# Graph attention on one core: the softmax denominators leave PSUM through ScalarE, and two VectorE steps change places

## The chip, the core and the metric

The kernel runs on one NeuronCore of a Trainium2 chip. A core has five engines that run side by side, each through its own instructions in order: TensorE (PE in the profile; matrix products, whose results go to PSUM), VectorE (DVE), ScalarE (ACT), GpSimd (POOL) and SyncE (SP, which here issues transfers). [...] The metric is the device time of one launch in microseconds (us), lower is better; before the change it is 3842.06 us, the median of three runs from 3838.66 to 3844.71.

## The reference

Two layers on 32 graphs of 512 nodes with 512 features. All graphs share one adjacency matrix `adj` (512 x 512, about 3% ones). Each layer adds something to its input and normalises the rows.

```python
# layer 0: message passing
deg = adj.sum(axis=1)
out = deg[None, :, None] * (x @ Wi.T + b) + einsum('ij,bjo->bio', adj, x @ Wj.T)
x = layernorm(x + out)

# layer 1: attention with 8 heads of 64, masked by adj
q, k, v = split_heads(h @ Wq.T + bq), split_heads(h @ Wk.T + bk), split_heads(h @ Wv.T + bv)
scores = where(adj == 0, -inf, einsum('bhqd,bhkd->bhqk', q, k) / 8)
out = einsum('bhqk,bhkd->bhqd', softmax(scores), v)       # heads merged again
x = layernorm(x + out @ Wo.T + bo)
```

The layer bias of layer 0 enters as `deg * b`, one row times one column.

## The kernel before

One program handles the graphs one after the other, with three of them in work at once: while the scores of graph `b` are computed, the attention output of `b-1` is projected, and layer 0 and the projections q, k, v of `b+1` are made. A period, one graph's worth of this, has eight score steps (two head groups of four key blocks). At each step TensorE computes the scores of two head pairs, the product with the values for the step before, and then a share of the projections, which come as "pieces" (L427) of sums and differences of quarters of the matrices.

**The softmax.** Scores are made with keys on the partitions, so the mask is a multiplication after the exponential, and the denominators are sums over partitions, done by TensorE with a matrix of ones:

```python
    def scores(b, hp, kc):
        ps = sc_tile()                                    # [128, 2, 512] in PSUM, bufs=2
        for s in range(2):
            r = slice(s * HD, (s + 1) * HD)
            nc.tensor.matmul(ps[:, s, :], KT[...][r, ...], QT[...][r, ...], start=True, stop=True)   # L481
        e = E[hp % 2, kc] = work([P, 2, N], "e", 4)
        nc.scalar.activation(ps, ps, AF.Exp, scale=QSCALE)                                           # L485
        nc.vector.tensor_tensor(e, ps, edge[...], op=OP.mult)                                        # L486

    def values(b, g, kc):                                 # L503: e times v, into PV[g], two banks "ov"
        ...
    def sums(g, kcs=(1,), last=1):
        if g not in RL:
            RL[g] = (sc_tile()[:, 0, :], work([P, N], "rl", 1))   # takes one of the two score tiles
        ...                                                       # L513: ones times es, into RL[g][0]

    def invert(g, part):
        pl, rl = RL[g]
        c = slice(part * P, (part + 1) * P)
        nc.vector.reciprocal(rl[:, c], pl[:, c])                                                     # L518

    def tell(b, g):
        pl, rl = RL.pop(g)
        j = b * 2 + g
        nc.vector.tensor_tensor_reduce(pl, pl, rl, 1.0, 0.0, OP.add, OP.add, told[:, j:j + 1])       # L523

    def scale(b, g, r, c=slice(0, N)):
        ...
        nc.vector.tensor_mul(OT[b, g][:, r, c], PV[g][r][:, c], RL[g][1][:, c])                      # L528

    def rest(b, g):
        return [(invert, g, c) for c in range(4)] + [(scale, b, g, 0), (scale, b, g, 1), (tell, b, g)]
```

`tell` adds up denominators and reciprocals, so that at the end the kernel can see whether a number ran out of range; a slower general path then takes over. The masked exponentials of the key blocks are added up ahead (`presum`: L492 on GpSimd, L494 on VectorE, tile `es`), so that the sums need one pass.

**Layer 0.** x arrives twice: in rows (`XT`) and in blocks that VectorE's transpose turns into columns (`XA`, turned into `XD`). The product with `adj` uses a split of x into two parts, made from `XT`:

```python
    def split(b, dc):
        xs = XT[b][:, :, dc * P:(dc + 1) * P]
        nc.scalar.copy(hi, xs)                                                                       # L203
        nc.gpsimd.tensor_sub(lo, xs, hi.bitcast(FT))                                                 # L204, tile xlo

    def l0_gather(b, dc, bank, adjT=None):                # L325: products, L331: copy out, then split(b, dc + 2)
        ...
    def l0_turn(b, dc):
        nc.vector.transpose(XD[b][:, dc, :], XA[b][:, dc, :])                                        # L339
        nc.gpsimd.tensor_tensor(XD[b][:, dc, :], XD[b][:, dc, :], deg_r, op=OP.mult)                 # L340

    def base(b, half):                                    # the layer bias, two blocks of rows
        for ic in range(2 * half, 2 * half + 2):
            y = XT[b][:, ic, :]
            nc.vector.scalar_tensor_tensor(y, b0_r, deg_c[:, ic:ic + 1], y, op0=OP.mult, op1=OP.add) # L345
```

**h.** The output of layer 0 goes to memory and comes back in blocks, to be turned in two halves; GpSimd forms differences of its quarters for the pieces:

```python
    def h_turn(b, half):
        nc.vector.transpose(HT[b][:, :, Q * half:Q * half + Q], HA[b][:, half])                      # L373, reads tile xa
    def combos(T, b, quarters, which, part=None):         # L396: GpSimd, tile big
        ...
```

**The order.** Lists of small functions lay down the order of a period; `g` are the gathers, `k` pieces of the k projection:

```python
    def phase_a(n):
        ...
        for i in range(DC):
            res += g[i:i + 1] + k[i:i + 1] + [z(l0_turn, n, i)]
            ...
        return res + [z(combos, TX, n, xq, (2,)), z(combos, TA, n, aq, (2,)), z(base, n, 0),
                      z(combos, TX, n, xq, (3, 4)), z(combos, TA, n, aq, (3, 4)), z(base, n, 1),
                      pc("l0", n, 1, A), k[4]]

    def phase_c(n):
        ...
            res = [z(apply, n, 1), z(h_store, n, 1), v[1], *project(m, 3), z(h_load, n, 1), z(stats, m, 0), v[2], z(stats, m, 1),
                   q[1], k[1], z(apply, m, 0), q[2], z(apply, m, 1), z(store, m), z(h_turn, n, 1),
                   z(combos, TH, n, h, (1, 2)), z(combos, TH, n, h, (3, 4)), k[2]]
```

The main loop puts them between the steps:

```python
        for step in range(STEPS):
            scores(b, 2 * g, kc)
            scores(b, 2 * g + 1, kc)
            ...
                values(pb, pg, pk)
                if pk == NC - 1:                          # the group's last key block
                    sums(pg)
                    extra = rest(pb, pg)
            ...                                           # then the pieces of this step, with `extra` between them
```

Of the kernel before, what the change touches and what calls it, by code (L numbers as in the profile page):

```python
# [9 lines left out]
FT = mybir.dt.float32  # L10
# [3 lines left out]
AF = mybir.ActivationFunctionType  # L14
OP = mybir.AluOpType
AX = mybir.AxisListType

P = 128
# [3 lines left out]
SAFE = 1e18  # L22
# [3 lines left out]
def gnn_attention_kernel(  # L26
# [36 lines left out]
    nc = tc.nc  # L63
    B, N, D = x.shape
# [8 lines left out]
    const = ctx.enter_context(tc.tile_pool(name="const", bufs=1))  # L73
# [6 lines left out]
    def work(shape, name, bufs, dtype=FT):  # L80
        return pools.work.tile(shape, dtype, name=name, bufs=bufs)

    def big():
        return work([P, 4, N], "big", 6)
# [7 lines left out]
    def sc_tile():  # L92
        return psum.tile([P, 2, N], FT, name="sc", bufs=2)
# [9 lines left out]
    TX, TA, TH, TO = {}, {}, {}, {}  # L103
# [68 lines left out]
    adj_f = big()  # L172
# [11 lines left out]
        return t  # L184


    told = const.tile([P, B * 2 + 1], FT, name="told")
    adjR = const.tile([P, NC, N], FR, name="adjR")
    adjT = turned(adj_f, big(), adjR)
    deg_r = const.tile([P, N], FT, name="deg_r")  # L190
# [35 lines left out]
    def graph_forms(part):  # L226
        if part == 3:
            nc.vector.reduce_sum(deg_c, adj_f, axis=AX.X)
        elif part == 0:
            nc.vector.tensor_tensor(adj_f, adjT, adjR.bitcast(FT), op=OP.not_equal)  # L230
        elif part == 1:
            nc.vector.reduce_sum(told[:, B * 2:], adj_f.rearrange("p c i -> p (c i)"), axis=AX.X)
            nc.vector.tensor_scalar(told[:, B * 2:], told[:, B * 2:], 2.0 * SAFE, None, op0=OP.mult)
        else:
            nc.vector.tensor_scalar(edge, adjT, 0.0, None, op0=OP.not_equal)

# [144 lines left out]
    def quarter(src, j, n):  # L381
        return src[:, 2 * j:2 * j + 2, Q * n:Q * n + Q]
# [92 lines left out]
    E, ES, PV, RL = {}, {}, {}, {}  # L475
# [30 lines left out]
    def sums(g, kcs=(1,), last=1):  # L506

        if g not in RL:
            RL[g] = (sc_tile()[:, 0, :], work([P, N], "rl", 1))
        for kc in kcs:  # L510
            for h in range(4):
                src = ES[h // 2] if kc == 1 else E[h // 2, kc]
                nc.tensor.matmul(RL[g][0][32 * h:32 * h + 32, :], ones[:, :32], src[:, h % 2, :], start=(kc == 1), stop=(kc == last))  # L513

    def invert(g, part):
        pl, rl = RL[g]
        c = slice(part * P, (part + 1) * P)
        nc.vector.reciprocal(rl[:, c], pl[:, c])  # L518

    def tell(b, g):  # L520
        pl, rl = RL.pop(g)
        j = b * 2 + g
        nc.vector.tensor_tensor_reduce(pl, pl, rl, 1.0, 0.0, OP.add, OP.add, told[:, j:j + 1])  # L523

    def scale(b, g, r, c=slice(0, N)):
# [4 lines left out]
    def rest(b, g):  # L530
        return [(invert, g, c) for c in range(4)] + [(scale, b, g, 0), (scale, b, g, 1), (tell, b, g)]
# [9 lines left out]
    def z(f, *a):  # L541
        return (0.0, f, *a)

    def pc(kind, b, i, bank):
        return (2 * PC if kind == "l0" else PC, piece, kind, b, i, bank)
# [6 lines left out]
    def banks(n):  # L552

        return ("a", "b") if n % 2 == 0 else ("b", "a")

    def phase_a(n):

        A, K = banks(n)
        if n == B:
            return [pc("k", n - 1, i, bank) for i, bank in ((6, K), (5, A), (7, K), (3, A), (4, K))]  # L560
        xq, aq = lambda j, m: quarter(XD[n], j, m), lambda j, m: quarter(AX_T[n], j, m)
        g = [(GA, l0_gather, n, dc, A) for dc in range(DC)]
        k = [pc("k", n - 1, i, K) for i in LATE]
        res = []
        for i in range(DC):
            res += g[i:i + 1] + k[i:i + 1] + [z(l0_turn, n, i)]
            if n == 1 and i in (1, 3):
                res += [z(combine, "wo", nc.vector, i // 2)]
            if i == 1:
                res += [z(combos, TX, n, xq, (1,)), z(combos, TA, n, aq, (1,))]  # L570
        return res + [z(combos, TX, n, xq, (2,)), z(combos, TA, n, aq, (2,)), z(base, n, 0),
                      z(combos, TX, n, xq, (3, 4)), z(combos, TA, n, aq, (3, 4)), z(base, n, 1),
                      pc("l0", n, 1, A), k[4]]

    def first():
# [25 lines left out]
    def project(m, i):  # L601

        res = [pc("pj", m, i, banks(m)[1])]
        if i == 1:
            res = [z(combos, TO, m, ot_quarter(m), (1,))] + res
        if i == 2:
            res = [FLUSH] + res + [z(combos, TO, m, ot_quarter(m), (2, 3, 4))]
        return res
# [21 lines left out]
    def phase_c(n):  # L630

        m = n - 2
        norm = [(TR, l0_norm, n, ic) for ic in range(NC)]
        h = lambda j, i: quarter(HT[n], j, i)
        A, K = banks(n)
        v, q, k = [{i: pc(kind, n, i, bank) for i in ORDER} for kind, bank in (("v", A), ("q", K), ("k", A))]
        if m < 0:
            res = [v[1]] + ([z(apply, n, 1)] if n else []) + [q[1], v[2], norm[2], norm[3], z(combos, TH, n, h, (1, 2)), k[1],
                                                             z(combos, TH, n, h, (3, 4)), q[2], k[2]]
        else:  # L640
            res = [z(apply, n, 1), z(h_store, n, 1), v[1], *project(m, 3), z(h_load, n, 1), z(stats, m, 0), v[2], z(stats, m, 1),
                   q[1], k[1], z(apply, m, 0), q[2], z(apply, m, 1), z(store, m), z(h_turn, n, 1),
                   z(combos, TH, n, h, (1, 2)), z(combos, TH, n, h, (3, 4)), k[2]]
        side = []
        if n == 0:

            side = [z(graph_forms, 2), None, z(graph_forms, 0), None, z(graph_forms, 1)]
        for i in LATE:
            for f in q[i], v[i]:
                res += [f] + [g for g in side[:1] if g]  # L650
                side = side[1:]
                if i in (6, 7) and 0 < n < B - 1:
                    res += [z(load_xa, n + 1, 2 * (i == 7) + (f is v[i]))]
            if i == 3 and 0 < n < B - 1:
                res += [z(load_x, n + 1)]
            if i == 7 and n + 1 < B:
                res += [z(ahead, n + 1)]
        return res
# [32 lines left out]
    def run(f):  # L691
        f[1](*f[2:])
# [49 lines left out]
    for n in range(1, B + 1):  # L742
        b = n - 1
        extra = []
        for step in range(STEPS):
            g, kc = divmod(step, NC)
            scores(b, 2 * g, kc)
            scores(b, 2 * g + 1, kc)
            pb, pg, pk = (b, *divmod(step - 1, NC)) if step > 0 else (b - 1, 1, NC - 1)
            if pb >= 0:  # L750
                values(pb, pg, pk)
                if pk == NC - 1:
                    sums(pg)
                    extra = rest(pb, pg)
            late = [(presum, i, kc) for i in range(2) if kc > 0]
            if b == B - 1 and kc == 3:
                late = [late[0], late[1] + (nc.gpsimd,)]
            if b == B - 1 and g == 1 and kc > 1:

                late = []  # L760
            for f in PERIODS[n][step]:
                if f is FLUSH:
                    some = len(extra)
                else:
                    run(f)

                    some = 0 if f[0] == 0.0 else len(extra) if step == 0 else max(1, round(f[0] / PC))
                if some:
                    for g in late[:1] + extra[:some]:
                        g[0](*g[1:])  # L770
                    late, extra = late[1:], extra[some:]
            for g in late + extra:
                g[0](*g[1:])
            extra = []
# [4 lines left out]
        last_part(c, 1)  # L779
    for ic in range(NC):  # L780
        c = slice(ic * P, (ic + 1) * P)
        invert(1, ic)
        scale(B - 1, 1, 0, c)
        scale(B - 1, 1, 1, c)
        last_part(2, ic=ic)
        last_part(3, ic=ic)
        if ic > 0:
            last_rows(ic - 1)
    tell(B - 1, 1)
    last_rows(NC - 1)  # L790
    flags()
    fast.close()
    flag = nc.values_load(again[0:1, 0:1], min_val=0, max_val=1)
    with tc.If(flag > 0), tc.tile_pool(name="general", bufs=1) as pools.work:
# [4 lines left out]
        adj_f = big()  # L799
# [21 lines left out]
        with tc.For_i(0, B, 1) as b:  # L821
            g = "general"
# [6 lines left out]
            for ic in range(NC):  # L829
                c = slice(ic * P, (ic + 1) * P)  # L830
# [10 lines left out]
            for ic in range(NC):  # L841
                c = slice(ic * P, (ic + 1) * P)
                nc.vector.tensor_copy(V[g][:, ic, :], product([(HT[g][:, dc, c], wv[:, dc, :]) for dc in range(DC)]))
            for hp in range(HP):
                c = slice(hp * P, (hp + 1) * P)
# [5 lines left out]
                for qb in range(NC):  # L851
# [7 lines left out]
                    for s in range(2):  # L859
# [3 lines left out]
                                            op0=OP.mult, op1=OP.add)  # L863
                    for s in range(2):
                        nc.scalar.activation(pr[:, s, :], pr[:, s, :], AF.Exp, bias=sm[:, 2 + s:3 + s], scale=1.0,
                                             accum_out=sm[:, 4 + s:5 + s])
# [14 lines left out]
            for ic in range(NC):  # L881
                c = slice(ic * P, (ic + 1) * P)
# [45 lines left out]
```

## Time and profile before

| | |
|---|---|
| time, median of three | 3842.06 us |
| span of the profiled execution | 3839.1 us |
| TensorE busy | 3695.2 us, 96% |
| VectorE busy | 2395.5 us, 62% |
| GpSimd busy | 1986.7 us, 52% |
| ScalarE busy | 992.5 us, 26% |
| mean granted clock of TensorE | 0.995 |

In the profile a line such as `PE sc L481 <- DVE told L523: 57.1, 32, 4.4` says: TensorE stood idle ahead of the products of line 481 that write tile `sc`, until VectorE's instruction of line 523 that writes `told` was done; 57.1 us in all, 32 times, at most 4.4 us. In a timeline the columns are start, length, engine, line, operation, output and inputs, shape and number; what stands in brackets is the idle time of the engine before it and who ended it. In a chain, which is followed back from the last instruction, they are start, length and work. `mma` and `mmb` are the two PSUM banks of the pieces, `ring` the tiles through which their weights come.

### The profile page before, as it was taken

Reading aid. Unit: us, or ns where it says so; the run is one execution under the profiler, and the core shown is the slowest. Engines: PE = TensorE matmul, PEld = TensorE weight load, DVE = VectorE, ACT = ScalarE, POOL = GpSimd, SP = SyncE. Lnnn points to the kernel's source line nnn. Section 1 sums busy time; section 2 is a strip of 40 time slices with the busy share of each in tenths; the row PEclk is TensorE's granted clock in tenths of the full one; section 3 lists DMA queues with packets and bytes.
Section 4 is the critical chain, followed back from the end, with each engine's and each line's share of the span. In section 5 each row is a group of like instructions: output and inputs, shape, how many; then the busy total and the mean of one; then the engine's idle time right before and its main releaser. Section 6 shows DMA issues by size and latency. Waiting matters only on the chain.

```text
span 3839.1 us, 49650 instructions
## 1 busy us (share of the span) xinstructions
PE 3695.2 (96%) x18458; PEld 2505.9 (65%) x18458; DVE 2395.5 (62%) x3202; ACT 992.5 (26%) x1356; POOL 1986.7 (52%) x1985
## 2 busy tenths in 40 slices
PE   8999999999999999999999999999999999999997
PEld 5666666666666666666666666666666666666663
DVE  4566666666666666666666666666666666666666
ACT  2222222222222222222222222222222222222222
POOL 3555545555445555455554555644555545555443
PEclk9999999999999999999999999999999999999999
DMA  7444555444554545554445544455544455444541
GB/s 246 133 114 129 138 151 154 129 129 132 140 157 139 132 125 143 147 155 129 127 131 149 151 135 128 131 143 154 144 126 130 139 150 154 128 126 133 145 131 46
DMA packets 797174, 530.03 MB, mean 138 GB/s; under 512 B 530432, under 2 KB 611840, under 8 KB 796928
## 3 DMA queue, kind: packets, MB, share of 16 engines
q1 hardware_dynamic: 780384, 494.78, 47.7%
q10 hardware_dynamic: 16320, 31.46, 2.2%
q8 instruction: 151, 2.47, 0.3%
q14 instruction: 95, 0.78, 0.1%
q0 software_dynamic: 224, 0.53, 0.0%
HBM read 453.25 MB, written 73.40 MB: 137 GB/s over the span
## 4 chain that ended last, share of the span: by engine, by line
PE 81%; DVE 15%; POOL 1%; SPq 1%; issue 1%; ACT 1%; DMA 0%; DVEq 0%; POOLq 0%; ACTq 0%
PE mma L427 27%; PE mmb L427 27%; PE sc L481 10%; PE ov L503 10%; DVE xh L345 4%; PE mmb L325 3%; PE mma L325 3%; DVE e L486 3%; DVE oT L528 1%; PE sc L513 1%; POOL big L396 1%; DVE es L494 1%; DVE big L373 1%; DVE rl L518 1%; ACT sc L485 1%
## 5 line engine op out<-in xcount | busy, mean ns | idle before, releaser
L485 ACT ACTIVATE sc<-sc 128x1024 f32<-128x1024 f32 x512 | 495.7, 1006 | 1703.1 <-PE sc L481 1697.4
L486 DVE TENSOR_TENSOR e<-sc,edge 128x1024 f32<-128x1024 f32 x512 | 604.9, 1217 | 341.1 <-ACT sc L485 315.6
L427 PE MATMUL mmb<-ring,big 128*128 128x256 f32 x3144 | 733.1, 382 | 3.1 <-issue 3.1
L427 PE MATMUL mma<-ring,big 128*128 128x256 f32 x3112 | 727.4, 382 | 4.2 <-ACT p L434 3.0
L427 PEld LDWEIGHTS mmb<-ring,big 128*128 128x128 f32 x3144 | 593.1, 190 | 133.8 <-issue 29.4
L427 PEld LDWEIGHTS mma<-ring,big 128*128 128x128 f32 x3112 | 587.4, 190 | 137.0 <-DVE e L486 26.8
L396 POOL TENSOR_TENSOR big<-big 128x512 f32<-128x512 f32 x376 | 508.1, 1378 | 163.7 <-DVE big L373 144.7
L481 PE MATMUL sc<-q,k 64*128 64x512 f32 x2048 | 521.0, 621 | 57.2 <-DVE told L523 57.1
L503 PE MATMUL ov<-e,v 128*32 128x512 f32 x4096 | 498.5, 605 | 0.0
L427 PE MATMUL mma<-big,ring 128*128 128x256 f32 x1808 | 431.8, 382 | 8.7 <-POOL big L396 8.0
L427 PE MATMUL mmb<-big,ring 128*128 128x256 f32 x1776 | 424.2, 382 | 8.5 <-POOL big L396 8.5
L492 POOL TENSOR_TENSOR es<-e 128x1024 f32<-128x1024 f32 x128 | 302.0, 2360 | 243.8 <-DVE e L486 240.7
L291 POOL TENSOR_SCALAR mv<-mv 128x1 f32<-128x1 f32 x256 | 51.0, 199 | 692.7 <-DVE mv L290 680.2
L427 PEld LDWEIGHTS mma<-big,ring 128*128 128x128 f32 x1808 | 339.2, 190 | 87.3 <-issue 13.8
L427 PEld LDWEIGHTS mmb<-big,ring 128*128 128x128 f32 x1776 | 333.2, 190 | 86.0 <-POOL big L396 14.5
L204 POOL TENSOR_TENSOR xlo<-xh,xhi 128x512 fp32r<-128x512 f32 x128 | 163.8, 1291 | 392.8 <-ACT xhi L203 392.8
L481 PEld LDWEIGHTS sc<-q,k 64*128 64x128 f32 x2048 | 174.6, 186 | 274.9 <-issue 270.3
L503 PEld LDWEIGHTS ov<-e,v 128*32 128x32 f32 x4096 | 107.8, 110 | 354.0 <-issue 354.0
L340 POOL TENSOR_TENSOR big<-big,deg_r 128x512 f32<-128x512 f32 x124 | 197.8, 1595 | 247.0 <-DVE big L339 247.0
L494 DVE TENSOR_TENSOR es<-es,e 128x1024 f32<-128x1024 f32 x251 | 306.8, 1223 | 0.0
L445 DVE TENSOR_TENSOR xh<-xh,mma 128x512 f32<-128x512 f32 x186 | 126.9, 682 | 272.4 <-PE mma L427 272.4
L445 DVE TENSOR_TENSOR xh<-xh,mmb 128x512 f32<-128x512 f32 x186 | 126.8, 682 | 257.9 <-PE mmb L427 257.7
(142 smaller groups left out, 3614.4 us busy)
## 6 DMA issues: line engine op xcount, KB each, us to landing
ring<-wo SPq DMA_DIRECT2D x217, 256.0 KB, 2.8
ring<-wq SPq DMA_DIRECT2D x160, 256.0 KB, 3.1
ring<-wv SPq DMA_DIRECT2D x160, 256.0 KB, 2.7
ring<-wk SPq DMA_DIRECT2D x160, 256.0 KB, 3.1
ring<-wi SPq DMA_DIRECT2D x155, 256.0 KB, 2.7
ring<-wj SPq DMA_DIRECT2D x155, 256.0 KB, 2.6
xh<-in_x_dram SPq DMA_DIRECT2D x32, 1024.0 KB, 5.3
xa<-in_x_dram SPq DMA_DIRECT2D x124, 256.0 KB, 4.0
```

Of the source, the lines that this page charges most:

```text
L204: nc.gpsimd.tensor_sub(lo, xs, hi.bitcast(FT))
L325: nc.tensor.matmul(pm, parts[w][:, jc, :], adjR[:, jc, :], start=(w == 0 and jc == 0), stop=(w == 1 and jc == NC - 1))
L340: nc.gpsimd.tensor_tensor(XD[b][:, dc, :], XD[b][:, dc, :], deg_r, op=OP.mult)
L396: nc.gpsimd.tensor_tensor(dst, p, q, op=OP.subtract)
L427: nc.tensor.matmul(pm[:, c * Q:(c + 1) * Q], lhs, rhs, start=first, stop=(kc == 1 and n == len(terms) - 1), skip_group_check=True)
L445: nc.vector.tensor_tensor(d, d, pm, op=OP.add)
L481: nc.tensor.matmul(ps[:, s, :], KT[b, hp // 2][r, hp % 2, kc * P:(kc + 1) * P], QT[b, hp // 2][r, hp % 2, :], start=True, stop=True)
L485: nc.scalar.activation(ps, ps, AF.Exp, scale=QSCALE)
L486: nc.vector.tensor_tensor(e, ps, edge[:, kc:kc + 1, :].to_broadcast([P, 2, N]), op=OP.mult)
L492: nc.gpsimd.tensor_add(ES[i], E[i, 0], E[i, 1])
L494: (eng or nc.vector).tensor_add(ES[i], ES[i], E[i, kc])
L503: nc.tensor.matmul(PV[g][r][32 * h:32 * h + 32, :], V[b][:, kc, c0:c0 + 32], E[h // 2, kc][:, h % 2, :], start=(kc == 0), stop=(kc == NC - 1))
```

## The change

Three things are moved, none of the mathematics.

1. The denominators are copied from PSUM to the tile `rl` by ScalarE as soon as TensorE has summed them (`drain`), with their sum as a by-product. The reciprocals are then taken in place in `rl`, and `tell` sums the reciprocals alone. The PSUM tile can go back to the scores after the copy. The last group of the last graph, where nothing follows, keeps the old way (`invert(..., 0)`, `tell_all`). `told` has two columns for each group now.
2. `base` stands after the transposes of chunks 1 and 2 of x, not after all four and GpSimd's differences.
3. `h_turn` of the second half stands ahead of a piece of q, which puts it in VectorE's order ahead of the masks of that step instead of behind them.

```diff
-    told = const.tile([P, B * 2 + 1], FT, name="told")
+    told = const.tile([P, B * 4 + 1], FT, name="told")
...
-    def invert(g, part):
-        pl, rl = RL[g]
+    def drain(b, g):
+
+        j = 2 * (b * 2 + g)
+        nc.scalar.activation(RL[g][1], RL[g][0], AF.Identity, accum_out=told[:, j:j + 1])
+
+    def invert(g, part, src=1):
         c = slice(part * P, (part + 1) * P)
-        nc.vector.reciprocal(rl[:, c], pl[:, c])
+        nc.vector.reciprocal(RL[g][1][:, c], RL[g][src][:, c])
 
     def tell(b, g):
+        j = 2 * (b * 2 + g) + 1
+        nc.vector.reduce_sum(told[:, j:j + 1], RL.pop(g)[1], axis=AX.X)
+
+    def tell_all(b, g):
+
         pl, rl = RL.pop(g)
-        j = b * 2 + g
+        j = 2 * (b * 2 + g)
+        nc.gpsimd.memset(told[:, j + 1:j + 2], 0.0)
         nc.vector.tensor_tensor_reduce(pl, pl, rl, 1.0, 0.0, OP.add, OP.add, told[:, j:j + 1])
...
             res += g[i:i + 1] + k[i:i + 1] + [z(l0_turn, n, i)]
+            if i in (1, 2):
+                res += [z(base, n, i - 1)]
...
-        return res + [z(combos, TX, n, xq, (2,)), z(combos, TA, n, aq, (2,)), z(base, n, 0),
-                      z(combos, TX, n, xq, (3, 4)), z(combos, TA, n, aq, (3, 4)), z(base, n, 1),
+        return res + [z(combos, TX, n, xq, (2,)), z(combos, TA, n, aq, (2,)),
+                      z(combos, TX, n, xq, (3, 4)), z(combos, TA, n, aq, (3, 4)),
                       pc("l0", n, 1, A), k[4]]
...
-                   q[1], k[1], z(apply, m, 0), q[2], z(apply, m, 1), z(store, m), z(h_turn, n, 1),
+                   q[1], k[1], z(apply, m, 0), z(h_turn, n, 1), q[2], z(apply, m, 1), z(store, m),
                    z(combos, TH, n, h, (1, 2)), z(combos, TH, n, h, (3, 4)), k[2]]
...
                     sums(pg)
+                    drain(pb, pg)
                     extra = rest(pb, pg)
...
-        invert(1, ic)
+        invert(1, ic, 0)
...
-    tell(B - 1, 1)
+    tell_all(B - 1, 1)
```

In the changed kernel the reciprocals have line 522, the drain 518, `tell`'s sum 526 and the scalings 538; lines up to 514 keep their numbers.

More of the change, by code (lines that the diff above doesn't have):

```diff
@@ L231, in graph_forms @@
         elif part == 1:
-            nc.vector.reduce_sum(told[:, B * 2:], adj_f.rearrange("p c i -> p (c i)"), axis=AX.X)
-            nc.vector.tensor_scalar(told[:, B * 2:], told[:, B * 2:], 2.0 * SAFE, None, op0=OP.mult)
+            nc.vector.reduce_sum(told[:, B * 4:], adj_f.rearrange("p c i -> p (c i)"), axis=AX.X)
+            nc.vector.tensor_scalar(told[:, B * 4:], told[:, B * 4:], 2.0 * SAFE, None, op0=OP.mult)
         else:
```

## The prediction

> **What bounds the kernel now.** I read the page's busy times and its chain first, then who TensorE waited for, then the timeline of one period (one of the 32 graphs; the score steps repeat every 117.6 us). TensorE is busy nearly all the time and makes up four fifths of the chain, so a change pays only where it fills a gap of TensorE:
>
> ```profile
> PE 3695.2 (96%) x18458; PEld 2505.9 (65%) x18458; DVE 2395.5 (62%) x3202; ACT 992.5 (26%) x1356; POOL 1986.7 (52%) x1985
> PE 81%; DVE 15%; POOL 1%; SPq 1%; issue 1%; ACT 1%; DMA 0%; DVEq 0%; POOLq 0%; ACTq 0%
> ```
>
> The view of the waits, for TensorE alone, names the gaps:
>
> ```profile
> PE sc L481 <- DVE told L523: 57.1, 32, 4.4
> PE sc L513 <- DVE e L486: 39.6, 31, 3.4
> PE mmb L427 <- POOL big L396: 8.5, 15, 0.6
> PE mma L427 <- POOL big L396: 8.0, 14, 0.6
> ```
>
> Three waits, each about once a period: 57.1 + 39.6 + 16.5 = 113.2 us of the 3839.1. Each belongs to one part of the change. Idle time is not yet the price, so I measured the steps. Here is TensorE's timeline where the first wait falls:
>
> ```profile
> 1826.47 1.13 PE L481 MATMUL sc<-q,k 64*128 64x512 f32 x4
> 1829.28 1.13 PE L481 MATMUL sc<-q,k 64*128 64x512 f32 x4 [1.67 <-DVE told L523]
> 1830.34 1.92 PE L503 MATMUL ov<-e,v 128*32 128x512 f32 x16
> 1832.19 1.99 PE L427 MATMUL mma<-big,ring 128*128 128x256 f32 x8
> ```
>
> From the first score product to the next projection it takes 1832.19 - 1826.47 = 5.72 us. An undisturbed step (1915.45 to 1919.22) takes 3.77. The wait costs 1.95 us, not 1.67. The chain, one period later, shows what it waits for:
>
> ```profile
> 1943.33 0.86 DVE rl L518
> 1944.19 0.68 DVE v L456
> 1944.87 1.19 DVE oT L528 x2
> 1946.07 0.61 DVE sc L523
> 1946.67 0.07 DVE told L523
> 1946.74 0.14 issue
> 1946.88 1.96 PE sc L481 x4
> ```
>
> The second score tile needs the PSUM buffer in which the denominators lie, and VectorE lets go of it only after the last reciprocal, both scalings and the sum for told. In this period the products after the wait are also slower (1.96 instead of 1.06). The view of stretches says why: the granted clock fell to 0.50 there.
>
> ```profile
> 1948.00:1950.00 2.00, 2.00 (x10) 0.40 (x12) 0.09 (x1) 1.11 (x2) 2.00 (x1) 0.50 0.59 226
> ```
>
> This step lasted 1944.07 to 1951.43, 7.36 us. Going through the told waits I find about five with such a low clock.
>
> [...] the bias addition of L345 lasts 706 to 1766 ns (median 1752), and of the four that start at 1986.7 the first, which begins ahead of GpSimd's L340, is the short one; the other three run beside L340 and the L396 subtractions. [...]
>
> **Part 1, the drain on ScalarE.** It adds 63 activations of 128x512 from PSUM with a sum. ScalarE's copy of that shape (L331) takes 586 ns; with the sum I estimate 0.6 to 0.8 us, 63 x 0.7 = 44 us on an engine that is 26% busy. It needs no new function: Identity and Exp already alternate and the trace has one table load. The sums of the first group ended at 1934.41, so the buffer comes free near 1935.3, and the next need for it is at 1945.2. The wait has 10 us of slack and goes. VectorE's part stays much the same: four reciprocals (now SBUF to SBUF, 924 ns before) and a plain sum in place of the 690 ns pass with its read-out. Could TensorE stop at the next order behind it? The products with the values need the old ov buffers, which the scalings of L528 free. They are free 1.40 and 2.0 us after the last projection ends (0.68 for L456, 0.6 for each scaling, with 0.1 of latency), and are needed 1.92 and 2.85 us after it. No. Gain: 32 x 1.95 = 62, about 3 more for the long one (4.4 us), and 5 x (7.36 - 5.72) = 8 for the clock: **73 us**.
>
> **Part 2, bias sooner.** In the chain the second group's sums wait behind the bias:
>
> ```profile
> 1986.77 5.67 DVE xh L345 x4
> 1992.44 0.13 DVE k L472
> 1992.57 0.19 issue
> 1992.76 0.47 DVE k L472
> 1993.23 1.14 DVE e L486
> 1994.37 0.04 issue
> 1994.41 1.07 PE sc L513 x8
> ```
>
> The exponentials of this step began at 1990.58, so the first mask could start at 1991.6, but VectorE is late by 1.6 us with 5.67 us of bias before it. This step takes 1995.41 - 1989.40 = 6.01 us; the same with sums but no wait (1929.78 to 1934.41) takes 4.63. Loss: 1.38 x 31 = **43 us**. In the new order two bias additions follow the second chunk's transpose and two the third's. The first pair must wait for GpSimd's last xlo (ends 1974.89; VectorE gets there at 1974.7), lasts up to 3.5 us and ends about 1978.4; the k addition behind it was due at 1976.8, its bank is needed at 1982.4, and the masks are due at 1978.9. The second pair runs from 1982.0 to about 1985; the next k addition then ends about 1986.5, and TensorE wants its bank at 1987.58. The last transpose ends about 1988.5 instead of 1986.8. So VectorE is idle again when the masks become possible, and the sums, due at 1993.2, have their buffer at 1992.8. All fits, with 0.4 to 1 us to spare. GpSimd's L396 for the next layer start some 1.5 us later; the second layer-0 product, which needs the first of them, comes near 2000, 7 us after they end.
>
> **Part 3, h turned first.** The transpose of 1.24 us stood behind the masks: 1934.27, and GpSimd's subtraction came out at 1936.92, when TensorE had waited 0.57 us. VectorE is idle from 1927.82 to 1931.99, before the masks. In the new order it turns there; h's second half landed at 1928.76, so it ends near 1930.0 and the subtraction near 1932.2. Gain: **16.5 us**. The landing is the danger: now VectorE waits for it with the masks behind it. Over the periods I compared the landing plus 1.24 us with the end of the first exponential: room of 1 to 2 us in most, 0.2 to 0.4 in five, a miss of 0.1 in one, and of several in the last period, whose loads are late already.
>
> **Sum.** 73 + 43 + 16.5 = 132 us if nothing comes back. I give back 8: 0.25 us a period for waits that were hidden behind these. 3842 - 132 + 8 = **3718 us** (3.2% less).
>
> **Rivals.** (a) *Another wait takes the place.* VectorE is the candidate, since its work is moved rather than removed and it stands in order: with q additions at 1939.0, 1942.45 and reciprocals between them it is just about full over 1939 to 1946. If every period gives back 1.5 us, 46 us return: about 3765. Against it: the slacks above come out positive one by one. (b) *The transfer of h sets the pace.* If it lands 2 us later than now, masks and sums wait, and 30 x 1 us or more come back: 3750 to 3765. For it: the thin room in six periods; against it: nothing in the change moves the store or the load against TensorE's products. (c) *Only part 1 works*, because the bias additions meet GpSimd and push the k additions into TensorE's way: 3842 - 73 - 16 = 3753, or 3780 if k is late twice a period. (d) *ScalarE becomes a wait*: the drain stands in order before the normalisation and k's bias at 1936.44, and waits for the sums till 1934.41. The two L296 (1.51 us) then end at 1936.7 instead of 1934.3, so k's bias is 0.3 us late, and its bank is not needed until 1938. Worth nothing, unless the sum costs ScalarE far more than the copy. None of the four alone makes the kernel slower than before.
>
> **Range and chances.** The lower end is all 132 us with a little more from the clock: 3704. The upper end is one rival at half strength: 3758. 2% is 76.8 us, so faster by over 2% means under 3765: it needs 58% of the sum. I put that at 0.84, within 2% at 0.14, slower at 0.02.
>
> **What would show it right or wrong.** Right: the told wait gone from TensorE's waits; the sums' wait on e under 8 us; none for POOL big in the q products; a period of 113.7 to 114.2 us instead of 117.6; granted clock 0.997 or more. Wrong in part 1: TensorE's scores or value products waiting for ScalarE or L538's scalings. Wrong in part 2: the products of L427 waiting for DVE k, or VectorE waiting for GpSimd's xlo. Wrong in part 3: VectorE's L373 waiting for the landing of xa from hd, and L513 behind it.

## The result, and the profile after

The changed kernel takes 3708.46 us (median of four runs, 3707.0 to 3709.89) against 3843.38 us of the kernel before on the same chip: a ratio of 0.9651, with a 95% interval from 0.9634 to 0.9668. That is 134.9 us less.

The page of the profile after has TensorE full and the chain made almost of it alone:

```profile
PE 3665.2 (99%) x18458; PEld 2511.4 (68%) x18458; DVE 2396.9 (65%) x3139; ACT 1029.1 (28%) x1482; POOL 1946.5 (53%) x1986
PE 96%; DVE 1%; SPq 1%; POOL 1%; DMA 0%; issue 0%; ACT 0%; POOLq 0%; DVEq 0%; ACTq 0%
```

VectorE has as much work as before (2396.9 us; 2395.5 before) and left the chain all the same: its share fell from 15% to 1%. What changed is when its work is done. The view of the waits of TensorE, longest first, shows what is left:

```profile
PE sc L180 <- DVE big L174: 5.5, 3, 4.1
PE sc L513 <- DVE e L486: 4.9, 1, 4.9
PE ov L736 <- DVE tot L734: 4.1, 1, 4.1
PE ov L503 <- DVE oT L538: 3.6, 2, 2.4
PE mma L427 <- DVE k L465: 3.2, 1, 3.2
```

No wait occurs more than three times. The three that came once a period are gone; what remains belongs to the start and to the last period. In between, the scores of one step begin at 2106.46 and those of the same step of the next graph at 2219.89, a period of 113.43 us where it was 117.60 (1826.47 to 1944.07); the prediction's sign was 113.7 to 114.2, so a little more was gained in each period than it counted.

The place of the first wait, now. The timeline has VectorE's last projection sum, the scalings and the sum for told, and TensorE's scores and value products:

```profile
2106.46 1.99 PE L481 MATMUL sc<-q,k 64*128 64x512 f32 x8
2106.56 0.69 DVE L456 TENSOR_TENSOR v<-mma,p 128x512 f32<-128x512 f32 x1
2107.17 1.28 DVE L538 TENSOR_TENSOR oT<-ov,rl 128x512 f32<-128x512 f32 x2
2108.37 0.68 DVE L526 TENSOR_REDUCE told<-rl 128x1 f32<-128x512 f32 x1
2108.37 1.92 PE L503 MATMUL ov<-e,v 128*32 128x512 f32 x16
```

All eight score products run in one piece and the value products follow at once; the step takes the 3.77 us of an undisturbed one. VectorE still finishes told after the scores have begun. It no longer matters, since the scores don't need its buffer.

### The profile page after: what moved, and what is told of

Read it like the earlier page. It is cut to its first block, busy times and chain, and to the rows that moved or that the text cites. A ratio compares the mean times of both kernels' runs of the same rounds, so it can differ in the third digit from the quotient of the medians.

```text
span 3706.9 us, 49623 instructions
## 1 busy us (share of the span) xinstructions
PE 3665.2 (99%) x18458; PEld 2511.4 (68%) x18458; DVE 2396.9 (65%) x3139; ACT 1029.1 (28%) x1482; POOL 1946.5 (53%) x1986
## 4 chain that ended last, share of the span: by engine, by line
PE 96%; DVE 1%; SPq 1%; POOL 1%; DMA 0%; issue 0%; ACT 0%; POOLq 0%; DVEq 0%; ACTq 0%
PE mma L427 31%; PE mmb L427 31%; PE sc L481 13%; PE ov L503 13%; PE mmb L325 3%; PE mma L325 3%; PE sc L513 2%; SPq L113 0%; DMA wv<-e 0%; DVE e L486 0%; DVE rl L522 0%; DVE st L289 0%; SPq L144 0%; PE sc L721 0%; SPq L166 0%
## 5 line engine op out<-in xcount | busy, mean ns | idle before, releaser
L427 PE MATMUL mmb<-ring,big 128*128 128x256 f32 x3144 | 733.7, 382 | 3.1 <-issue 3.1
L427 PE MATMUL mma<-ring,big 128*128 128x256 f32 x3112 | 724.5, 381 | 3.9 <-ACT p L434 2.8
L427 PEld LDWEIGHTS mmb<-ring,big 128*128 128x128 f32 x3144 | 593.7, 190 | 134.1 <-issue 30.2
L427 PEld LDWEIGHTS mma<-ring,big 128*128 128x128 f32 x3112 | 585.7, 190 | 135.6 <-issue 27.0
L481 PE MATMUL sc<-q,k 64*128 64x512 f32 x2048 | 509.7, 616 | 0.0
L396 POOL TENSOR_TENSOR big<-big 128x512 f32<-128x512 f32 x376 | 493.1, 1339 | 29.3 <-ACT big L354 10.1
L503 PE MATMUL ov<-e,v 128*32 128x512 f32 x4096 | 494.0, 600 | 3.6 <-DVE oT L538 3.6
L427 PE MATMUL mma<-big,ring 128*128 128x256 f32 x1808 | 431.5, 382 | 3.2 <-DVE k L465 3.2
L427 PE MATMUL mmb<-big,ring 128*128 128x256 f32 x1776 | 422.7, 381 | 0.0
L427 PEld LDWEIGHTS mma<-big,ring 128*128 128x128 f32 x1808 | 341.0, 190 | 76.8 <-issue 25.1
L427 PEld LDWEIGHTS mmb<-big,ring 128*128 128x128 f32 x1776 | 334.5, 190 | 72.0 <-issue 25.1
L503 PEld LDWEIGHTS ov<-e,v 128*32 128x32 f32 x4096 | 107.1, 109 | 351.6 <-issue 321.7
L340 POOL TENSOR_TENSOR big<-big,deg_r 128x512 f32<-128x512 f32 x124 | 174.0, 1404 | 266.5 <-DVE big L339 266.5
```

Of the source, the lines that this page charges most:

```text
L396: nc.gpsimd.tensor_tensor(dst, p, q, op=OP.subtract)
L427: nc.tensor.matmul(pm[:, c * Q:(c + 1) * Q], lhs, rhs, start=first, stop=(kc == 1 and n == len(terms) - 1), skip_group_check=True)
L481: nc.tensor.matmul(ps[:, s, :], KT[b, hp // 2][r, hp % 2, kc * P:(kc + 1) * P], QT[b, hp // 2][r, hp % 2, :], start=True, stop=True)
L503: nc.tensor.matmul(PV[g][r][32 * h:32 * h + 32, :], V[b][:, kc, c0:c0 + 32], E[h // 2, kc][:, h % 2, :], start=(kc == 0), stop=(kc == NC - 1))
```

## The experiments

All times are medians; "before" is the kernel before, run beside them on the same chip. Its median differs by up to 3.7 us from one such comparison to the next (3839.69 to 3843.38), so smaller differences between kernels of different comparisons mean little. "Refill" in the expectations is the 0.2 to 0.3 us by which a step with a wait lasts longer than without, beyond the idle time itself (1.95 against 1.67 us for the told wait).

**Each part alone.** Three kernels, each the kernel before with one part of the diff (the drain with its `invert` and `tell`; the two `base` lines; the place of `h_turn`).

> Part 1 alone on the kernel before. My theory (the three waits are separate, and each part removes one): the told wait (57.1 us) goes, with its refill and the low clock behind it; 69 us less than before, so about 3774 us (3766 to 3782). The sums' wait on e stays near 39.6 us and the one on POOL big near 16.5. Rival (the waits hide one another): without the told wait VectorE is late elsewhere, another wait takes 20 us or more, and the time stays above 3790.

> Part 2 alone. Theory: the sums' wait on e falls from 39.6 us to under 3, 43 us less than before: about 3799 us (3792 to 3806), told and POOL big as before. Rival (the bias additions meet GpSimd at their new place and make the k additions late): a wait of L427 on DVE k or of L325 appears and less than 30 us remain.

> Part 3 alone. Priced as in the prediction, by idle time alone: 16.5 us, so about 3825 us. Theory after the result: each of these waits also costs a refill of 0.26 us, as the step lengths suggest (2.56 us instead of 1.73 for the piece), so 30 x 0.83 = 25 us and about 3817. Rival (the landing of h now holds the masks): an L513 wait on e appears and 3830 or more.

| kernel | time, us | before, us | less by |
|---|---|---|---|
| drain only | 3774.06 | 3841.16 | 67.1 |
| bias only | 3795.95 | 3841.16 | 45.2 |
| turn only | 3821.41 | 3841.16 | 19.8 |
| sum of the three | | | 132.1 |
| all three (the changed kernel, run again) | 3707.57 | 3839.69 | 132.1 |

The parts add up. Each removes its own wait and leaves the others nearly as they were (with the drain alone the sums' wait on e is 42.2 us in all, 39.6 before); the longest waits of TensorE in the bias-only kernel:

```profile
PE sc L481 <- DVE told L523: 57.1, 32, 4.4
PE mmb L427 <- POOL big L396: 8.5, 15, 0.6
PE mma L427 <- POOL big L396: 8.0, 14, 0.6
```

The wait on e is down to one of 3.1 us in the last period, the other two stand to the tenth as before. So the rival that the waits hide one another falls. The turn-only kernel lies between its two expectations, 16.5 and 25 us. Its own step behaved as the second of them says: the typical period is 116.77 us, 0.82 less. But the told waits, which it keeps, were followed by a low clock more often: 11 of the 32 in its profile, 6 in the kernel before; of the 29 that last 1.67 us, 10 and 4. Its mean granted clock is 0.992 (0.995 before), and a period with a low clock in it is 1.64 us longer. Six more of these are 10 us, which leaves about 14 of the 24 that this kernel's shorter step is worth; the spans of the two profiles differ by 15.0 (the profiled execution, 3825.8 us, is the longest of the four). Why the low clock came more often in this kernel stays open. One of these periods in its timeline:

```profile
2056.05 1.97 PE L481 MATMUL sc<-q,k 64*128 64x512 f32 x4 [1.67 <-DVE told L523]
2057.95 2.73 PE L503 MATMUL ov<-e,v 128*32 128x512 f32 x16
2060.61 1.99 PE L427 MATMUL mma<-big,ring 128*128 128x256 f32 x8
```

The same idle time of 1.67 us as in the other steady periods, and here the four score products take 1.97 us and not 1.13.

**Is ScalarE needed?** The prediction priced the drain by the time at which the buffer comes free. If that is all, an earlier release by VectorE itself must do as well. The edit takes the reciprocals straight from PSUM and leaves the denominators' own sum out of the range test:

```diff
-    def invert(g, part, src=1):
+    def invert(g, part, src=0):
...
-                    drain(pb, pg)
```

> The changed kernel without the drain: the reciprocals read PSUM again, and tell sums the reciprocals alone, so the denominators' own sum is left out of the range test. Then the score buffer comes free with the last reciprocal, some 1.9 us before the scalings and tell would have ended. Theory A (only the time of release counts, and the last reciprocal is early enough, 1 us ahead of the need): same time as the changed kernel, 3708 us within 6, no wait of the scores. Theory B (the bank has to leave VectorE's hands altogether): a wait of the scores on DVE rl of 0.5 us or more a period, 3725 us or more.

It takes 3706.58 us: as fast as with the drain. Its waits on the reciprocals come from the last period:

```profile
PE sc L481 <- DVE rl L522: 2.2, 2, 1.6
```

So Theory A holds. The gain of part 1 is not the speed of ScalarE's copy, nor work taken from VectorE (busy 2397.1 us here and 2395.5 before; `tell` alone got shorter, by 0.15 us); it is that the two scalings and the sum for told no longer stand between the last reciprocal and the release of the PSUM tile. What the drain buys beyond this kernel is the denominators' sum, which it makes as it copies.

**How much room has VectorE?** Two needless sums of `rl` (1.4 us together) between the reciprocals and the scalings:

```diff
+    def again_sum(b, g):
...
+        for _ in range(2):
+            nc.vector.reduce_sum(told[:, j:j + 1], RL[g][1], axis=AX.X)
...
-        return [(invert, g, c) for c in range(4)] + [(scale, b, g, 0), ...
+        return [(invert, g, c) for c in range(4)] + [(again_sum, b, g)] + [(scale, b, g, 0), ...
```

> The changed kernel with two more sums of rl on VectorE between the reciprocals and the scalings (work added, nothing else changed). They take about 1.25 us. Theory (VectorE has about 0.6 us to spare there, the scalings end 0.6 us before the value products need the buffer): TensorE waits for DVE oT about 0.65 us a period, with the refill 0.9, so 32 x 0.9 = 29 us more than the changed kernel: about 3737 us (3725 to 3747). Rival (VectorE has room, being busy 65%): no change, 3708 within 4.

It takes 3772.61 us, 65 us more than the changed kernel, more than twice what I expected. The waits of TensorE name two places, not one:

```profile
PE ov L503 <- DVE oT L538: 28.3, 32, 2.6
PE mmb L427 <- issue: 17.8, 16, 3.1
PE mma L427 <- issue: 13.8, 14, 1.0
```

The first is the one that I had worked out (28.3 us of idle time). The second is put down to "issue", that is to nothing that the profile can name. The timeline of this kernel, after the second head group, shows what it is:

```profile
2197.41 1.41 DVE L543 TENSOR_REDUCE told<-rl 128x1 f32<-128x512 f32 x2
2198.73 1.28 DVE L538 TENSOR_TENSOR oT<-ov,rl 128x512 f32<-128x512 f32 x2
2199.48 0.30 PEld L427 LDWEIGHTS mma<-ring,oT 128*128 128x128 f32 x2 [1.35 <-issue]
2199.51 2.11 PE L427 MATMUL mma<-ring,oT 128*128 128x256 f32 x8 [0.98 <-issue]
2200.06 1.16 PEld L427 LDWEIGHTS mma<-ring,oT 128*128 128x128 f32 x6 [0.28 <-DVE oT L538]
```

The product reads `oT`, the tile that the scalings write, as its weights: the load of the weights waits, and the product behind it. The first of the two scalings ends at 2199.41 and the first load begins at 2199.48, though its own wait too is put down to "issue"; the later loads name the scalings. In the changed kernel the same place has almost nothing to spare; the first scaling ends at 2161.30, and the first load begins at 2161.37:

```profile
2160.61 1.29 DVE L538 TENSOR_TENSOR oT<-ov,rl 128x512 f32<-128x512 f32 x2
2161.37 0.39 PEld L427 LDWEIGHTS mma<-ring,oT 128*128 128x128 f32 x2
2161.57 1.95 PE L427 MATMUL mma<-ring,oT 128*128 128x256 f32 x8
2161.95 1.16 PEld L427 LDWEIGHTS mma<-ring,oT 128*128 128x128 f32 x6 [0.19 <-DVE oT L538]
```

Two more kernels put the sums in one group only (`range(2 if g == 0 else 0)`, and the same with 1), to see whether this accounts for the whole:

> The changed kernel with the two more sums in the first head group alone. If the place that the prediction named (value products behind the scalings) is half of what the two sums cost: a wait of L503 on DVE oT of 0.8 us a period, 0.85 with refill, about 27 us more than the changed kernel's 3707.6: 3735 us (3729 to 3741), and no wait of L427. Rival (the two groups hang together, and the cost comes only with both): under 10 us.

> The changed kernel with the two more sums in the second head group alone. Theory: the other half of the cost is a place the prediction missed, where the second piece of the output projection reads the tiles that the scalings write; there TensorE has nothing to spare. A wait of L427, put down to issue, of 1.0 us a period, 1.3 with refill: about 38 us more, 3746 us (3738 to 3752), and no wait of L503. Rival: under 10 us.

They take 3733.36 and 3745.42 us: 25.8 and 37.8 us more than the 3707.57 of the changed kernel. The sum is 63.6 of the 65.0. The first has the wait of L503 and none of L427 on "issue" beyond the one of 3.1 us that all kernels have; the second the reverse (of L503 only two in the last period, 3.7 us in all, as in the changed kernel). The first line is of the first kernel, the others of the second:

```profile
PE ov L503 <- DVE oT L538: 27.9, 32, 3.4
PE mmb L427 <- issue: 17.8, 16, 3.1
PE mma L427 <- issue: 13.8, 14, 1.0
```

Both expectations held. VectorE is busy 65% of the time and yet cannot take 1.4 us more at either place.

**How much room has the landing of h?** The load of the second half is issued one piece later:

```diff
-... *project(m, 3), z(h_load, n, 1), z(stats, m, 0), v[2], z(stats, m, 1),
+... *project(m, 3), z(stats, m, 0), v[2], z(h_load, n, 1), z(stats, m, 1),
```

> The changed kernel with the load of h's second half issued one piece later (about 1.7 us). Theory: VectorE already waits for this landing in 30 periods, with a mean of 1.1 us to spare before the masks; 1.7 us later uses that up in most periods: an L513 wait on e of 0.4 to 0.8 us in some 25 of them, with refill about 20 us in all, about 3729 us (3716 to 3742). Rival (the landing has more room than it seems, because the queue gets free earlier): under 4 us, 3708 to 3712.

3723.0 us, 15.4 more than the changed kernel. The wait that part 3 put at risk appears:

```profile
PE sc L513 <- DVE e L486: 12.6, 13, 4.9
```

VectorE's own wait for the landing grew from 48.1 us in all (30 times) in the changed kernel to 101.5, so 1.8 us a period; in 12 periods it reached TensorE, with 7.7 us of idle time (12.6 less the 4.9 of the last period, which the changed kernel has too). With the refill that is some 11 of the 15.4 us. The rest isn't shown to come from the edit: in the two profiles 3.3 us of the difference are there before the first score step, and some 2 us arise in the last period; the mean granted clock is 0.995 here and 0.997 in the changed kernel.

I had expected some 25 periods and 20 us. The rival is wrong, and my size was too big. In the changed kernel VectorE is idle between the turn and the masks for 0 to 1.8 us, 1.1 on average over 29 periods; here that idle time is 0.07 us at most in all of them. So the delay used up VectorE's room everywhere, but in 17 periods the sums could still take what lateness was left.

**The last period.** The sums' wait of 4.9 us that is left comes from layer-norm statistics of the last graph but one, which stand ahead of the masks. Moved back by more than a step (with the changed kernel again beside it):

```diff
-[p[3], p[4], z(stats, m, 0), z(stats, m, 1)], [z(apply, m, 0), z(apply, m, 1), z(store, m)], [own[0]], [own[1]], []]
+[p[3], p[4]], [], [own[0], z(stats, m, 0), z(stats, m, 1)], [own[1], z(apply, m, 0), z(apply, m, 1), z(store, m)], []]
```

> The changed kernel with the layer-norm statistics of the last but one graph moved one step and more back in the last period, out from under the masks. Theory: the sums' wait of 4.9 us in the last period goes, and with it the low clock behind it: 5 to 8 us less than the changed kernel, about 3701 us. Rival (the end of the kernel is a chain of VectorE steps, where they now stand in the way): no gain, or a loss of up to 3 us.

> The changed kernel again, as the companion of the run before on the same chip: 3708 us within 3.

The wait fell from 4.9 us to 1.6, and a new one of 1.2 us of the scores on the masks appears further on. The time is 3705.09 us (3704.31 to 3707.94) against 3707.57 (3705.59 to 3709.47): 2.5 us lower, less than the 5 to 8 I expected, and the two ranges overlap. Both lie clearly below the kernel before (ratios 0.9652 and 0.9656). It has the lowest median of the versions that leave nothing out, but its lead over the changed kernel isn't shown. The value products' wait for the scalings, 2.4 and 1.8 us in the two profiles of the changed kernel, is 3.0 here:

```profile
PE sc L513 <- DVE e L486: 1.6, 1, 1.6
PE sc L481 <- DVE e L486: 1.2, 1, 1.2
PE ov L503 <- DVE oT L538: 4.2, 2, 3.0
```

## Why the prediction was right

The time, 3708.5 us, lies inside the range of 3704 to 3758 and 10 us under the predicted 3718. The reason held too, though some of the closeness is luck: part 1 came out 4 us smaller than predicted and part 3 almost 8 us larger. The sizes, step by step:

**Part 1, predicted 73 us.** Alone it is worth 67.1. Added over all 32, the steps with the told wait shrank from 196.0 to 126.6 us, 69.3. Two terms were too large. At the end of the last period the told wait of 4.4 us went, but the value products wait 2.4 us for the scalings instead; that step fell from 9.85 us to 8.47 only, 1.4 us where 5 were counted. And the low clock lengthened four of the steady periods (119.23 instead of 117.6 us), not five. One was too small: a wait of 2.6 us earlier in the last period was counted like the others, and its step fell by 3.2 us. The two waits of the value products for the scalings, 1.2 and 2.4 us, are what the prediction had named as a sign against part 1; they come in the last period alone. In the steady periods the estimate of slack was right: the two scalings run from 2107.17 to 2108.45, the value products that need the first of them begin at 2108.37, and none waits. The drain takes 598 ns and 194 for reading out its sum, 0.79 us, at the upper end of the estimate and without effect.

**Part 2, predicted 43.** Alone 45.2. In the 30 periods before the last one its step shrank from 182.4 to 138.9 us in all, 43.5, and a low clock (0.50 from 227 to 229 us) behind the first and longest of these waits (3.38 us) went with it, 1.7 more. VectorE's order came out as worked by hand. Its timeline in the changed kernel:

```profile
2133.72 3.42 DVE L345 SCALAR_TENSOR_TENSOR xh<-b_r,deg_c,xh 128x512 f32<-128x512 f32 x2 [0.21 <-POOL xlo L204]
2137.06 0.68 DVE L465 TENSOR_TENSOR k<-mma,k 128x512 f32<-128x512 f32 x1
2137.69 2.36 DVE L486 TENSOR_TENSOR e<-sc,edge 128x1024 f32<-128x1024 f32 x2
2140.59 2.40 DVE L345 SCALAR_TENSOR_TENSOR xh<-b_r,deg_c,xh 128x512 f32<-128x512 f32 x2
2150.42 2.36 DVE L486 TENSOR_TENSOR e<-sc,edge 128x1024 f32<-128x1024 f32 x2 [1.23 <-ACT sc L485]
```

The wait for GpSimd's xlo is there (0.21 us; worked out as 0.19, though the same prediction lists such a wait as a sign against part 2), the first pair lasts 3.42 us (estimate 3.5), the second 2.40 (3.0), and before the last masks VectorE is idle for 1.23 us until ScalarE has the exponentials. The bias additions are as long as ever (1463 ns on average, 1479 before); they only stand where nothing waits for them. The first graph is the exception, and there the prediction's other sign against part 2 came: two bias additions stand ahead of other work of VectorE and a k addition, and the products wait 3.17 us for it. The first line is of the kernel before, the second of the changed one:

```profile
106.62 1.99 PE L427 MATMUL mma<-big,ring 128*128 128x256 f32 x8 [0.73 <-DVE k L465]
108.66 3.14 PE L427 MATMUL mma<-big,ring 128*128 128x256 f32 x8 [3.17 <-DVE k L465]
```

**Part 3, predicted 16.5.** This was mis-sized, and against the prediction's own words that idle time is not the price. It priced the first two waits by the length of their steps and this one by its idle time. The timeline of the kernel before has the piece and its wait:

```profile
1934.41 1.99 PE L427 MATMUL mma<-big,ring 128*128 128x256 f32 x8
1936.97 1.99 PE L427 MATMUL mmb<-big,ring 128*128 128x256 f32 x8 [0.57 <-POOL big L396]
```

The piece takes 1934.41 to 1936.97 = 2.56 us, where such a piece takes 1.73 without a wait: 0.83 us, 29 times, so 24. The turn-only kernel's period says the same, 0.82. In the run it brought 19.8, because of the low clock that came along with the waits it kept; with those gone in the full change, all 0.83 are there: 1.95 + 1.38 + 0.83 = 4.16 us a period, and the period fell by 4.17.

**The 8 us given back** did not come in the steady periods, but nearly all of them came at the two ends. The first graph is 3.3 us longer in the profile after, most of it the wait for the k addition (3.17 us instead of 0.73). In the last period the sums' step is 3.3 us longer than before (10.61 against 7.30). Taken together: 69.3 + 45.2 + 24.1 - 3.3 - 3.3 = 132.0 us. The spans of the two profiles differ by 132.2, where 124 were predicted. The medians differ by 134.9, since the profiled run of the kernel before (3840.86 us) was 2.5 us faster than the median of this comparison.

**The rivals.** (a) No other wait took the place in the steady periods, but the room was as thin as feared, and thinner at a place that the prediction didn't look at: the scalings of the second group feed the projection at once, where the changed kernel has some 0.15 us to spare (an estimate: of the 1.41 us of added sums, 37.8 / 30 = 1.26 a period reached the time). (b) VectorE does wait for h to land, 48.1 us in 30 periods:

```profile
2093.36 1.25 DVE L373 STREAM_TRANSPOSE big<-xa 128x1024 f32<-128x1024 f32 x1 [2.14 <-DMA xa<-hd]
2095.21 2.36 DVE L486 TENSOR_TENSOR e<-sc,edge 128x1024 f32<-128x1024 f32 x2 [0.60 <-ACT sc L485]
```

It waits 2.14 us, turns, and is idle for another 0.60 before the masks are possible: here the landing is hidden behind the exponential. This room is 1.1 us on average, and none in one period. (c) came once, in the first graph, where the k addition was late; (d) did not come.

## What to carry to other kernels

Where one engine is nearly full and waits a little in every period, price each wait by the length of the step it sits in, against the same step without it, and not by the idle time alone; here 1.67 us of idle time cost 1.95, and 0.57 cost 0.83. Ask of each wait what the last use of the buffer really is: a PSUM tile was held through two scalings that didn't read it and a sum that read it for a side result, which cost 1.7% of this kernel, and a release before them, by ScalarE or by VectorE, gave that back. Before adding work to an engine that looks 65% busy, look at the instructions that the full engine needs next at that very point: the same 1.4 us cost 26 us at one place and 38 at another.

## What the runs showed of the hardware

- A halved TensorE clock (granted clock 0.50 from 1948 to 1950 us in the kernel before) followed only some of the told waits. Of the 29 that left TensorE idle for the same 1.67 us, 4 were followed by one in the kernel before and 10 in the turn-only kernel. Of the 29 sums' waits of 1.17 us, none was, in either kernel. What decides which of these waits it follows was not shown.
- A reciprocal of 128x128 took 924 ns from PSUM (L518 before) and 926 from SBUF (L522 after), longer than a sum (L526, 676 ns), a product (L538, 683 ns) or an addition (L456, 691 ns) of 128x512, four times the size.
- The sum that came with the drain's activation cost ScalarE an instruction of its own, 194 ns on average of 63; the drain took 598 ns besides, a plain copy of the same shape (L331) 586.
- With the two sums, the product that waited for its weights to be written appeared in the waits of TensorE as "issue" (0.98 us at 2199.51), and so did its first weight load (1.35 us). Only the loads behind it (PEld, 0.28 us at 2200.06) named the scalings.
